# Adjacency layer kernel: row-shaped loads for all tiles, last weights in parts, and four smaller edits

## Chip, cores and metric

The kernel runs on one core of a Trainium2 chip. The metric is the device time of one execution in microseconds (us), as the median of several runs. A core has five engines with queues of their own: PE (TensorE, matrix products), DVE (VectorE), ACT (ScalarE), POOL (GpSimd) and SP (SyncE, which here only issues transfers). Transfers between HBM and the on-chip memory SBUF are carried by 16 DMA engines. Products of PE land in PSUM, which has eight banks of 2 KB a partition.

## What is computed

The reference, cut to what matters. x is (4096, 64), adj is (4096, 4096) with zeros and ones in float32 (64 MiB), and the weight is (64, 64).

```python
h = jnp.maximum(_layernorm(x, axis=-1), 0.0)
support = h @ weight
mask = (adj != 0).astype(support.dtype)
rank = jnp.cumsum(mask, axis=1)
deg = rank[:, -1:]
k = jnp.minimum(deg, 100.0)
pos = rank - (deg - k)
w = mask * jnp.where(pos > 0, 0.5 ** (k - pos), 0.0)
out = x + w @ support + bias
```

A neighbour's weight is thus one half to the power of the number of neighbours that stand behind it in its row, and zero where the row has 100 or more behind it.

## The kernel before

The 4096 rows of adj are cut into 32 tiles of 128 rows (row tile t, one row to each partition, 16 KB a row, 2 MiB a tile). Each goes through a chain of stages, and the tiles overlap in it. The stages, with the function's name, its engine and its line:

1. `load` (SP): row tiles 0 to 29 come as 128 partitions by 16 KB (L307; tile 0 in two halves). Tiles 30 and 31 come "by columns": each of four transfers fills 32 partitions with pieces of 4 KB (L311), twelve transfers in all, since tile 31 is further cut in two.
2. `convert` (DVE, L509) turns the float32 mask into bytes, four to a word. `flip` (DVE, L520 for rows, L525 for columns) transposes 32x32 blocks of words, so that neighbours lie along partitions.
3. `totals` (PE, L532) counts neighbours by blocks, `split` (ACT, L538) takes the two bytes of each count, `suffix` (PE, L551) adds up the counts of the blocks behind with the constant matrices near, rest, far and past. `clamp` (DVE, L556) limits them.
4. `place` (PE, L565 and L570) builds in four PSUM banks (pool v) a word for each neighbour whose bytes are the exponents. `weigh` (ACT, L584) takes the exponential: four instructions a tile, j = 0 to 3, 1024 values a partition each, into the buffer wk, which holds a unit of two tiles.
5. `aggregate` (PE, L601) multiplies hr by a unit's weights: 32 products of 128x256 a unit, in eight tasks of four, accumulated in the one bank of pool acc. hr is the support in two parts, `first` (ACT, L489) and the remainder, `second` (DVE, L492), so that the result has two halves of 64 rows.
6. Every two units (four tiles): `drain` (ACT, L611, for the last part DVE, L613) adds the bias, `turn_back` (PE, L619) transposes 128x128 blocks, `finish` (DVE, L626 and L627) adds the two halves to x in two additions, `store` (SP, L631) writes the rows.

Ahead of the tiles stands a set-up: `fetch` (x), `turn`, `center`, `square`, `relu`, `spread` for the layer norm, `root` (DVE, L462 to L464) and `power` (POOL, L469 to L474, three Newton steps) for the reciprocal root, `support` and `scale` (DVE, L482). `constants` and `order_of` (DVE, L388 to L420) build the constant matrices near, rest, far and where; `count` needs near.

The order on each engine is fixed when the kernel is built. `tasks()` lists every call with its engine, what it needs, how long it holds the engine, and a due time from the table DUE. `plan()` simulates the engines and always takes, of the tasks that can start soon, the one with the smallest due time. The calls are then written out in that order, and every engine works through its own list strictly in order. `pool` entries are PSUM or SBUF buffers: NA = 4 buffers of adj tiles, NV = 5 banks for v, NB = 2 banks for t (which holds tot, ps and po in turn), one bank for acc. A load needs the convert of the tile four before it. `warm` issues products of zeros (L431) where the plan has PE idle before `spread`.

Of the kernel before, what the change touches and what calls it, by code (L numbers as in the profile page):

```python
# [8 lines left out]
F32 = mybir.dt.float32  # L9
# [6 lines left out]
U8 = mybir.dt.uint8  # L16
# [14 lines left out]
UNITS = [("rows", ((t, 0, 4), (t + 1, 0, 4))) for t in range(0, 30, 2)] + [("columns", ((30, 0, 4), (31, 0, 2), (31, 2, 4)))]  # L31
SPANS = {"rows": 8, "columns": 2}
STEP = {0: 2}
U = len(UNITS)
PIECES = [(u, i) for u, (_, pieces) in enumerate(UNITS) for i in range(len(pieces))]
LOADS = []
for u, i in PIECES:
    t, g0, g1 = UNITS[u][1][i]
    step = STEP.get(t, g1 - g0)
    LOADS += [(u, i, k, k + step) for k in range(g0, g1, step)]  # L40
DRAINS = [(g, 0, 4, True) for g in range(7)] + [(7, 0, 2, True), (7, 2, 3, True), (7, 3, 4, False)]
STORES = [(0, 0, 16), (1, 0, 12), (1, 12, 14), (1, 14, 15), (1, 15, 16)]
NA, NM, NT, NW, NV, NB = 4, 4, 4, 2, 5, 2

DUE = {
    "fetch": [-686, -126],
    "load": [724, 583, 273, 792, 448, 655, 939, 650, 1013, 730, -119, 964, 1305, 584, 218, 814, 1129, 955, 149, 993, 40,
    765, 956, 78, 684, 958, 306, 922, 424, 450, 164, 71, 1115, 730],
    "load_rest": [-204],
    "turn": [359, 315, 260, 710, 487, 222, 133, -266],  # L50
    "turned": [-185, -335, 64, -727, -1045, -251, -968, -881],
    "center": [360, -58, 207, -35],
    "square": [-87, -1268, -175, 619],
    "relu": [-239, 514, 1391, -334],
    "spread": [-680, -580, -580, 15],
    "support": [21, 24, 95, 42],
    "scale": [861, -308, -468, -124],
    "root": [844],
    "power": [174],
    "constants": [-220, -1059],  # L60
    "order_of": [1056],
    "count": [1111],
    "counted": [10],
    "first": [-514, -397, -30, -113],
    "second": [-417, 143, 783, 704],
    "convert": [482, 1025, 204, 226, 727, 309, 981, 1114, 367, 687, 1132, 1067, 867, 1749, 1371, 1701, 256, 1583, 1540,
    856, 1257, 1456, 1412, 1612, 1915, 1541, 2485, 1819, 1871, 2184, 1807, 1638, 1616, 2086],
    "flip": [-114, 308, 291, 923, 674, -114, 690, 807, -100, 831, 543, 437, 630, 1887, 1255, 1800, 979, 1228, 961, 744,
    1153, 1971, 1323, 1552, 1990, 1126, 1724, 1289, 2088, 1984, 2223, 1296, 1905, 2123],
    "totals": [-3, 552, -46, 841, 433, 189, 81, 601, 415, -464, -591, 136, 611, 1280, 503, 1008, 578, 335, 987, 424,  # L70
    685, 602, 1305, -158, 1197, 1439, 1190, 839, 1469, 919, 1061, 1251, 1091],
    "split": [761, 727, 1045, 717, 751, 769, -156, 772, 17, 1132, 865, 862, 499, 667, 955, 987, 1510, 1187, 1234, 350,
    1194, 1337, 750, 878, 1289, 1830, 1061, 1369, 1498, 1532, 1176, 1109, 1727],
    "suffix": [183, 405, -150, 111, 631, -317, 930, 770, 128, 167, 1286, 587, 1533, 512, 1005, 852, 704, 676, 956, 1751,
    1680, 1362, 1491, 577, 1388, 1268, 1495, 1814, 1765, 1130, 1431, 1709, 2042],
    "clamp": [321, 347, 443, 415, 222, 598, 567, 424, 121, 506, 857, 749, 466, 653, 638, 701, 1299, 997, 674, -57, 972,
    1295, 1419, 477, 1910, 863, 1576, 1079, 584, 801, 1235, 1277, 1913],
    "place": [-25, 778, 16, 550, 117, -32, 40, -6, 92, 41, -143, 48, 468, -231, -158, 1140, 356, 68, 498, 801, 768,
    1322, 971, 1992, 893, 1057, 834, 1829, 1233, 1823, 1881, 1472, 1293],
    "weigh": [-539, -10, 974, 122, -11, -72, 83, 150, 27, 775, 317, 129, -832, -333, -51, 636, 535, 294, 532, 123, 180,  # L80
    378, 466, -70, 639, 222, 730, 838, 795, 370, 3, 64, 752, 536, 729, 774, 139, 88, 559, 654, 785, 582, 88, 787, 1053,
    118, 807, 706, 489, 825, 591, 69, 761, 655, 427, 704, 340, 743, -9, 457, 789, 281, 1115, 479, 792, 1172, 665, 313,
    1129, 1711, 790, 1140, 1070, 953, 1054, 509, 1453, 384, 1493, 842, 315, 782, 467, 940, 983, 1433, 1265, 954, 1411,
    876, 1666, 1502, 1255, 848, 803, 1220, 1400, 1237, 1021, 1867, 1311, 858, 1342, 1376, 1740, 1425, 1760, 1471, 2210,
    1505, 1441, 1561, 1791, 1838, 1656, 2274, 2036, 1458, 1383, 852, 799, 1464, 848, 1978, 1179, 1428, 1547, 1352, 796,
    2201, 1653, 1588],
    "aggregate": [405, 292, 97, 611, -155, 1241, -31, 842, 332, 334, 1114, 914, 1063, 882, 706, 826, 632, 748, 1116,
    423, 423, 679, 89, 819, 525, 722, 392, 807, 611, 1238, 1392, -269, 1280, 824, 135, 740, 1044, 980, 682, 959, 368,
    650, 826, 977, 447, 432, 945, 564, 860, 911, 943, 1550, 795, 1481, 1191, 503, 690, 693, 824, 516, 1094, 676, 1580,
    2035, 1092, 1330, 876, 1281, 1390, 1259, 1542, 2317, 1637, 1016, 1566, 1168, 1392, 1083, 962, 1526, 1048, 1123,  # L90
    1190, 1017, 661, 1207, 2606, 1891, 1494, 1205, 1663, 1458, 782, 2062, 1503, 2022, 1500, 2071, 2003, 1841, 1219,
    1977, 1613, 827, 1835, 2025, 1748, 1355, 1745, 1953, 2096, 2431, 899, 2009, 1570, 1701, 1819, 1985, 2681, 1641,
    1109, 2260, 2265, 2409, 2272, 1848, 924, 1875],
    "drain": [64, 247, 512, 1185, 1142, 1625, 1534, 1794, 1955, 2201],
    "turn_back": [1333, 1555, 2261, 2462, 2286, 2762, 2419, 1952, 2550, 2777],
    "finish": [403, 912, 821, 1212, 1760, 2467, 1688, 2395, 2803, 2383],
    "store": [10242, 11508, 11343, 11289, 10767],
# [3 lines left out]


def width(u, i):
    _, g0, g1 = UNITS[u][1][i]
    return 64 * (g1 - g0)


def offset(u, i):
    return sum(width(u, k) // 2 for k in range(i))


def tasks():
# [9 lines left out]
    at, when = 6.0, {}  # L122
    for u, i in PIECES:
        at += width(u, i) * 5 / 256
        when[u, i] = at
    for r in range(2):
        task("fetch", (r,), SP, 0.5, 0, 0, [])
    def tile_of(n):
        u, i = LOADS[n][:2]
        return UNITS[u][1][i][0]  # L130

    for n in range(len(LOADS)):
        task("load", (n,), SP, n, 0, 0, [("convert", m) for m in range(n) if tile_of(m) == tile_of(n) - NA])
# [15 lines left out]
    task("power", (), POOL, 3, 2600, 2700, [("root",)])  # L149
    task("constants", (0,), DVE, 0, 600, 650, [])  # L150
    task("constants", (1,), DVE, 6, 1700, 1750, [])
    task("order_of", (), DVE, 1, 1200, 1250, [("constants", 0)])
# [5 lines left out]
    for n, (u, i, k0, k1) in enumerate(LOADS):  # L158
        k = k1 - k0
        due = when[u, i]  # L160
        hold = 622 * k + 20
        task("convert", (n,), DVE, due, hold, hold + 170, [("load", n)], ("b", ("flip", n)))
        hold = 268 * k + (60 if UNITS[u][0] == "rows" else 120)
        o = PIECES.index((u, i))
        task("flip", (n,), DVE, due + 2, hold, hold + 120, [("convert", n)] + ([("place", *PIECES[o - NT])] if o >= NT else []))
    for u, i in PIECES:
        kind, pieces = UNITS[u]
        due, w = when[u, i] + 3, width(u, i)
        task("totals", (u, i), PE, due, 470 * w // 512 + 95, 470 * w // 512 + 315, [("flip", n) for n, part in enumerate(LOADS) if part[:2] == (u, i)], ("t", ("split", u, i)))
        task("split", (u, i), ACT, due + 0.5, 2 * w * 833 // 1000 + 50, 2 * w * 833 // 1000 + 190, [("totals", u, i)])  # L170
        hold = (650 if kind == "rows" else 350) * w // 256
        task("suffix", (u, i), PE, due + 1, hold, hold + 220, [("split", u, i)], ("t", ("clamp", u, i)))
        task("clamp", (u, i), DVE, due + 1.5, w * 1042 // 1000 + 125, w * 1042 // 1000 + 245, [("suffix", u, i), ("counted",)])
        hold = 750 if w == 256 else 650
        task("place", (u, i), PE, due + 2, hold, hold + 220, [("clamp", u, i), ("constants", 1)], ("v", *[("weigh", u, i, j) for j in range(4)]))
        for j in range(4):
            hold = 4 * w * 833 // 1000 + 52
            needs = [("place", u, i)] + ([("second", j) for j in range(4)] if u == 1 else [])
            task("weigh", (u, i, j), ACT, due + 3 + j, hold, hold + 140, needs, ("w", ("aggregate", u, 7)) if i == j == 0 else None)
# [68 lines left out]
def kernel(  # L248
# [9 lines left out]

    nc = tc.nc
    P = 128
# [415 lines left out]
```

## Time and profile before

| what | us |
|---|---|
| median of 3 runs | 198.77 (198.32 to 198.81) |
| the profiled execution, own time | 200.25 |
| its span in the profile | 198.0 |
| PE busy | 164.3 |
| ACT busy | 153.3 |
| DVE busy | 152.1 |
| POOL busy | 9.9 |
| q1, the queue of the loads and stores, share of 16 DMA engines | 88.0% |

The span is the stretch that the profile's records cover; the execution's own time holds 2.25 us more around it. Busy times of an engine count its instructions from start to end, and neighbouring instructions overlap by some tenths of a us, so that four weigh instructions of 1.05 us mean take 3.77 us in a row. The mean granted clock of PE over the span is 0.914 of full speed.

### The profile page before, as it was taken

How to read it: one execution, taken by the hardware profiler on the slowest of the kernel's cores; microseconds unless marked ns; L12 is line 12 of the kernel's file. 1: busy time of each engine (PE TensorE's matmuls, PEld its weight loads, DVE VectorE, ACT ScalarE, POOL GpSimd, SP SyncE). 2: the span in 40 equal slices, each digit the busy share in tenths (PEclk: the TensorE clock that was granted, in tenths of full speed). 3: DMA queues.
4: the chain of work that ended last, by engine and by line, in shares of the span. 5: the costliest groups of instructions: out<-in, count | busy, mean ns of one | idle time of the engine just before them, and what ended most of it. 6: DMA issues, size and time to landing. Idle time of an engine off the chain costs nothing.

```text
span 198.0 us, 4612 instructions
## 1 busy us (share of the span) xinstructions
PE 164.3 (83%) x2007; PEld 124.3 (63%) x2007; DVE 152.1 (77%) x169; ACT 153.3 (77%) x195; POOL 9.9 (5%) x46
## 2 busy tenths in 40 slices
PE   7899882698965998898988898998988978568992
PEld 5775571386753776676666776785866755445881
DVE  4876869996996988979988689999989845664212
ACT  2863468385938997999999999989999996286650
POOL 7000820000000000000000000000000000000000
PEclk9995599559999999999999999999999996965899
DMA  6999999999999999999999999999999999830020
GB/s 221 405 434 424 440 424 406 437 427 427 427 420 424 422 430 420 427 424 434 424 424 417 430 417 427 427 430 424 430 417 391 199 223 223 243 118 3 0 93 13
DMA packets 6947, 69.52 MB, mean 351 GB/s; under 512 B 1296, under 2 KB 1424, under 8 KB 2960
## 3 DMA queue, kind: packets, MB, share of 16 engines
q1 hardware_dynamic: 6768, 69.21, 88.0%
q8 instruction: 15, 0.25, 0.5%
q10 hardware_dynamic: 160, 0.03, 0.1%
q14 instruction: 4, 0.03, 0.1%
HBM read 68.19 MB, written 1.05 MB: 350 GB/s over the span
## 4 chain that ended last, share of the span: by engine, by line
PE 37%; DMA 22%; DVE 17%; ACT 15%; POOL 3%; issue 3%; SPq 1%; POOLq 0%; ACTq 0%; DVEq 0%
PE acc L601 22%; DMA a_sb<-in_adj_dram 22%; ACT wk L584 12%; DVE m L509 8%; PE ps L551 5%; DVE mt L520 4%; PE v L570 3%; PE v L565 3%; PE tot L532 3%; DVE behind L556 2%; POOL t L473 2%; ACT sums L538 1%; PE po L619 1%; ACT acc_sb L611 1%; DVE wk L482 1%
## 5 line engine op out<-in xcount | busy, mean ns | idle before, releaser
L584 ACT ACTIVATE wk<-v 128x1024 fp32r<-128x1024 uint8 (+1 forms) x132 | 123.0, 1029 | 13.7 <-PE v L570 12.6
L509 DVE TENSOR_SCALAR m<-a_sb 128x4096 uint8<-128x4096 f32 (+1 forms) x34 | 84.0, 2479 | 13.4 <-DMA a_sb<-in_adj_dram 13.4
L601 PE MATMUL acc<-wk,hr 128*128 128x256 f32 x512 | 78.1, 304 | 6.2 <-ACT wk L584 5.4
L601 PEld LDWEIGHTS acc<-wk,hr 128*128 128x128 f32 x512 | 68.6, 203 | 14.6 <-ACT wk L584 7.6
L520 DVE STREAM_TRANSPOSE mt<-m 128x1024 f32<-128x1024 f32 (+1 forms) x31 | 37.1, 1203 | 0.3
L538 ACT ACTIVATE sums<-tot 128x512 f16<-128x512 uint8 (+1 forms) x33 | 20.0, 607 | 14.2 <-PE tot L532 7.8
L556 DVE TENSOR_SCALAR behind<-ps,excess 128x256 f16<-128x256 f32 (+1 forms) x33 | 15.5, 470 | 19.0 <-PE ps L551 17.1
L565 PE MATMUL v<-behind,where 32*128 32x256 f16 (+1 forms) x264 | 16.8, 281 | 12.1 <-DVE behind L556 8.7
L532 PE MATMUL tot<-mt,band 128*32 128x256 f16 (+1 forms) x264 | 14.3, 300 | 4.6 <-DVE mt L520 3.1
L551 PEld LDWEIGHTS <-far_rows 128*128 128x128 f16 x210 | 17.3, 103 | 1.2
L565 PEld LDWEIGHTS <-where 32*128 32x128 f16 x264 | 5.9, 93 | 19.2 <-issue 16.5
L551 PE MATMUL ps<-sums,far_rows 128*128 128x224 f16 (+6 forms) x210 | 17.8, 228 | 0.0
L570 PE MATMUL v<-mt,tri 32*32 32x512 f16 (+1 forms) x528 | 15.3, 413 | 0.0
L551 PE MATMUL ps<-sums,near 128*128 128x256 f16 (+1 forms) x33 | 9.7, 293 | 4.7 <-ACT sums L538 4.6
L532 PEld LDWEIGHTS <-band 128*32 128x32 f16 x264 | 4.4, 97 | 11.4 <-issue 5.3
L570 PEld LDWEIGHTS <-tri 32*32 32x32 f16 x528 | 4.6, 88 | 7.2 <-issue 7.0
L551 PE MATMUL ps<-sums,rest_rows 128*128 128x256 f16 x30 | 8.6, 287 | 0.0
L611 ACT ACTIVATE acc_sb<-acc,bias_sb 128x512 f32<-128x512 f32 (+2 forms) x9 | 5.8, 644 | 2.8 <-PE acc L601 2.7
L551 PEld LDWEIGHTS <-near 128*128 128x128 f16 x33 | 3.5, 105 | 5.6 <-issue 3.4
L458 PEld LDWEIGHTS pd<-ones,wk 128*128 128x128 f32 x32 | 5.0, 234 | 1.8 <-ACT wk L449 1.3
L619 PE MATMUL po<-ident,acc_sb 128*128 128x128 f32 x31 | 5.1, 282 | 1.0 <-ACT acc_sb L611 1.0
L449 ACT ACTIVATE wk<-pc 128x512 f32<-128x512 f32 x4 | 2.4, 600 | 4.6 <-PE pc L446 4.6
(93 smaller groups left out, 87.7 us busy)
## 6 DMA issues: line engine op xcount, KB each, us to landing
a_sb<-in_adj_dram SPq DMA_DIRECT2D x29, 2048.0 KB, 13.8
a_sb<-in_adj_dram SPq DMA_DIRECT2D x2, 1024.0 KB, 8.6
a_sb<-in_adj_dram SPq DMA_DIRECT2D x4, 512.0 KB, 19.1
a_sb<-in_adj_dram SPq DMA_DIRECT2D x8, 256.0 KB, 11.9
xr<-in_x_dram SPq DMA_DIRECT2D x2, 512.0 KB, 3.8
out_dram<-xr SPq DMA_DIRECT2D x1, 512.0 KB, 7.4
out_dram<-xr SPq DMA_DIRECT2D x1, 384.0 KB, 2.3
out_dram<-xr SPq DMA_DIRECT2D x1, 64.0 KB, 1.7
```

What stands on the lines that cost most here:

```text
L509: nc.vector.tensor_scalar(m_v, a_v, 0.0, 64.0, op0=ALU.not_equal, op1=ALU.add)
L520: nc.vector.transpose(to.rearrange("p c (h r) -> p h c r", r=SUB)[:, 2 * k0:2 * k1], m_v)
L532: nc.tensor.matmul(tot[SUB * c:SUB * (c + 1), :w], band[:, SUB - 12 - 4 * a:2 * SUB - 12 - 4 * a], masks[u, i][:, c, :w, a], start=(a == 0 ...
L538: nc.scalar.activation(sums8[u, i][:, :, :w], pts.pop((u, i, "n"))[:, :w].bitcast(U8).rearrange("p (i f) -> p f i", f=4)[:, :2, :], AF.Cop ...
L551: nc.tensor.matmul(o, l, m, start=(k == 0), stop=(k == len(todo) - 1), skip_group_check=True)
L556: nc.vector.tensor_scalar(behind[u, i][:, :w], pts.pop((u, i, "s"))[:, :w], excess, float(MAX_NEIGH), op0=ALU.subtract, op1=ALU.min)
L565: nc.tensor.matmul(vs[u, i, j][:, a * w:(a + 1) * w], where[q, a, :], behind[u, i][q, :w], start=(a == 0), stop=False, skip_group_check=True)
L570: nc.tensor.matmul(vs[u, i, j][SUB * c:SUB * (c + 1), :2 * w], tri[q, q], masks[u, i][q, c, :w, :].rearrange("p i a -> p a i"), start=Fals ...
L584: nc.scalar.activation(to, v, AF.Exp, scale=-LN2, bias=-38.0 * LN2)
L601: nc.tensor.matmul(accs[g][:, at:at + 2 * P], hr[:, b, :, :].rearrange("p s d -> p (s d)"), w, start=(k == m == 0), stop=(k == 7 and m == ...
L611: nc.scalar.activation(sums[d][:, :w], accs[g][:, i0 * P:i1 * P], AF.Identity, bias=bias_sb)
L619: nc.tensor.transpose(pts["o", d][:, k, :, :].rearrange("p s d -> p (s d)"), sums[d][:, k * P:(k + 1) * P], ident)
```

## The change

Six things differ.

- All 32 tiles are loaded by rows. Tiles 0, 1 and 28 to 31 come in two halves of 1 MiB (8 KB a row), the others whole. The column form goes with everything that served it: L311, the second form of flip, rest and far in two versions.
- The weights of tile 31 are made in three parts: for each j one instruction of 512 values, then one of 256, then one of 256 (PARTED), and the aggregates of the last unit each need only the part that they read. An aggregate task now takes one (a, s) and four h.
- `power` moves from POOL to DVE, nine instructions in place of thirteen. `constants(1)` and `order_of` move from DVE to POOL.
- `warm` is called ahead of any task: where the plan has PE idle and PE's recent work in a stretch of 3.4 us is small, products of zeros are put in, which add nothing to the accumulator in use.
- `turn_back` multiplies by the matrix `both` (two identities of 64 on top of each other), which transposes and adds the two halves in one product, so `finish` is one addition. The last drains and stores are cut in two pieces in place of three, and all drains are on ACT.
- Buffers: NV = 6 and NB = 1 in place of 5 and 2; two buffers for sums in place of one. The table DUE is new, and so is the order on every engine.

```diff
-UNITS = [("rows", ((t, 0, 4), (t + 1, 0, 4))) for t in range(0, 30, 2)] + [("columns", ((30, 0, 4), (31, 0, 2), (31, 2, 4)))]
-STEP = {0: 2}
-DRAINS = [(g, 0, 4, True) for g in range(7)] + [(7, 0, 2, True), (7, 2, 3, True), (7, 3, 4, False)]
-STORES = [(0, 0, 16), (1, 0, 12), (1, 12, 14), (1, 14, 15), (1, 15, 16)]
-NA, NM, NT, NW, NV, NB = 4, 4, 4, 2, 5, 2
+TILES = range(32)
+STEP = {t: 4 for t in (0, 1, 28, 29, 30, 31)}
+LOADS = [(t, h, h + STEP.get(t, 8)) for t in TILES for h in range(0, 8, STEP.get(t, 8))]
+PARTLY = {31}
+PARTED = (0, 1, 0, 2), (1, 2, 0, 1), (1, 2, 1, 2)
+DRAINS = [(g, 0, 4, True) for g in range(7)] + [(7, 0, 2, True), (7, 2, 4, True)]
+STORES = [(0, 0, 16), (1, 0, 12), (1, 12, 14), (1, 14, 16)]
+NA, NM, NT, NW, NV, NB = 4, 4, 4, 2, 6, 1
...
     def load(n):
...
-        if kind == "rows":
-            nc.sync.dma_start(tiles[t][:, k0 * N // 4:k1 * N // 4], adj_v[:, t // HT, t % HT, k0 * N // 4:k1 * N // 4])
-        else:
-            to = tiles[t].rearrange("(q p) (g n) -> q p g n", q=E, g=E)
-            for q in range(E):
-                nc.sync.dma_start(to[q, :, k0:k1, :], quarters[t // HT, t % HT, q, :, k0:k1, :])
+        nc.sync.dma_start(tiles[t][:, k0 * W:k1 * W], adj_v[:, t // HT, t % HT, k0 * W:k1 * W])
...
     def power():
         y, t, v = ns["y"], ns["t"], ns["v"]
-        nc.gpsimd.tensor_scalar(v, v, -0.5, None, op0=ALU.mult)
         for i in range(3):
-            nc.gpsimd.tensor_tensor(t, y, y, op=ALU.mult)
-            nc.gpsimd.tensor_tensor(t, t, v, op=ALU.mult)
-            nc.gpsimd.tensor_scalar(t, t, 1.5, None, op0=ALU.add)
-            nc.gpsimd.tensor_tensor(y, y, t, op=ALU.mult)
+            nc.vector.tensor_tensor(t, y, y, op=ALU.mult)
+            nc.vector.scalar_tensor_tensor(t, v, -0.5, t, op0=ALU.mult, op1=ALU.mult)
+            nc.vector.scalar_tensor_tensor(y, t, 1.5, y, op0=ALU.add, op1=ALU.mult)
...
+    idle = [ps_a.tile([P, W], F32, tag="acc", name="none"), 2 * P]
     def warm(n):
-        for i in range(n):
-            nc.tensor.matmul(none[:, :2 * P], junk[:, :P], junk, start=True, stop=True)
+        for i in range(n if idle else 0):
+            nc.tensor.matmul(idle[0][:, idle[1]:idle[1] + 2 * P], junk[:, :P], junk, start=not accs, stop=not accs, skip_group_check=True)
...
-    def weigh(u, i, j):
+    def weigh(t, j, part=0):
...
+        a0, a1, s0, s1 = PARTED[part] if t in PARTLY else (0, 2, 0, 2)
+        v = vs[t, j].rearrange("p a i -> p (a i)").bitcast(U8).rearrange("p (x r f) -> p f x r", f=4, r=SUB)
+        nc.scalar.activation(wts[u][:, s0:s1, 8 * a0:8 * a1, i, j, :], v[:, s0:s1, 8 * a0:8 * a1], AF.Exp, scale=-LN2, bias=-38.0 * LN2)
...
     def turn_back(d):
...
-            nc.tensor.transpose(pts["o", d][:, k, :, :].rearrange("p s d -> p (s d)"), sums[d][:, k * P:(k + 1) * P], ident)
+            nc.tensor.matmul(pts["o", d][:, k, :], sums[d][:, k * P:(k + 1) * P], both, start=True, stop=True)
...
     def finish(d):
...
-        nc.vector.tensor_add(o, po[:, :i1 - i0, 0, :], o)
-        nc.vector.tensor_add(o, po[:, :i1 - i0, 1, :], o)
+        nc.vector.tensor_add(o, pts.pop(("o", d))[:, :i1 - i0, :], o)
...
-    end = 1200
-    for at, hold, on_pe, f, args in plan():
-        if on_pe:
-            if end is not None and at - end > 700:
-                warm(int(at - end) // 215)
-            end = None if f == "spread" or end is None else at + hold
+    for at, spare, f, args in plan():
+        warm(spare)
         does[f](*args)
```

In plan(), the number of zero products ahead of a PE task:

```python
idle = 0
if engine == PE:
    recent = sum(rows for when, rows in spent if when > at - 3400)
    idle = max(0, min(int((at - end) * 0.6) // 110, (4200 - recent) // 256))
    spent += [(at, rows_of(f, args) + 256 * idle)]
    end = at + hold
```

## The prediction

> **What bounds the kernel now.** I read the slices first, for stages. One slice is 4.95 us.
>
> ```profile
> PEclk9995599559999999999999999999999996965899
> DMA  6999999999999999999999999999999999830020
> GB/s 221 405 434 424 440 424 406 437 427 427 427 420 424 422 430 420 427 424 434 424 424 417 430 417 427 427 430 424 430 417 391 199 223 223 243 118 3 0 93 13
> ```
>
> The reader is to see two things: all 16 DMA engines are busy to slice 36, but from slice 32 they move half as much, and behind the last byte lie four and a half slices with no load at all. The windows put numbers to it (columns: PE, PEld, DVE, ACT, POOL busy us and instructions, granted clock, DMA share, GB/s):
>
> ```profile
> 0.00:150.00 150.00, 128.84 (x1591) 96.27 (x1591) 127.75 (x137) 121.77 (x153) 9.93 (x46) 0.93 1.00 418
> 150.00:177.00 27.00, 20.66 (x254) 16.08 (x249) 18.02 (x16) 20.56 (x25) 0.00 (x0) 0.89 0.91 231
> 177.00:198.00 21.00, 14.80 (x168) 11.99 (x167) 6.36 (x17) 10.95 (x19) 0.00 (x0) 0.81 0.08 27
> ```
>
> Stage one: 150 us of stream at 418 GB/s (425 once it runs, in 60 to 150 us). Stage two: 27 us at 231 GB/s. Stage three: 21 us of work behind the last load. The queue of SP issues its first transfer by columns (L311) at 146.87, just before the rate falls. Next, VectorE's timeline, for when data is taken up: L509 converts a tile as soon as it may.
>
> ```profile
> 59.55 2.63 DVE L509 TENSOR_SCALAR m<-a_sb 128x4096 uint8<-128x4096 f32 x1
> ...
> 116.25 2.64 DVE L509 TENSOR_SCALAR m<-a_sb 128x4096 uint8<-128x4096 f32 x1
> ...
> 149.16 2.61 DVE L509 TENSOR_SCALAR m<-a_sb 128x4096 uint8<-128x4096 f32 x1
> ...
> 161.03 2.63 DVE L509 TENSOR_SCALAR m<-a_sb 128x4096 uint8<-128x4096 f32 x1 [3.24 <-DMA a_sb<-in_adj_dram]
> ...
> 169.90 2.63 DVE L509 TENSOR_SCALAR m<-a_sb 128x4096 uint8<-128x4096 f32 x1 [3.95 <-DMA a_sb<-in_adj_dram]
> ...
> 177.30 1.37 DVE L509 TENSOR_SCALAR m<-a_sb 128x2048 uint8<-128x2048 f32 x1 [1.91 <-DMA a_sb<-in_adj_dram]
> ```
>
> These are tiles 9, 20, 27, 29, 30 and the last half of 31. Between 22 and 157 us no convert waits for data; from tile 29 on each does. Last, the chain of waits (start, us, what), which names the end:
>
> ```profile
> 148.19 21.58 DMA a_sb<-in_adj_dram
> 169.79 7.38 DMA a_sb<-in_adj_dram
> ...
> 177.30 1.37 DVE m L509
> ...
> 189.54 4.07 PE acc L601 x32
> ```
>
> So what sets the end is the arrival of the last two tiles, and then a tail of 198.0 - 177.3 = 20.7 us.
>
> **The change, part by part.** *(1) Rows in place of columns.* The 12 transfers of L311 go; tiles 28 to 31 come in eight of 1 MB with 8 KB rows. By 150 us 150 x 0.418 = 62.7 MB are in; adj and x are 68.2 MB (the page's HBM read). The other 5.5 MB at 425 GB/s take 12.9 us: all bytes by 162.9. Landing is seen later than bytes: tile 1 is complete by bytes at 14.7 us and its convert, waiting for nothing else, starts at 16.7. With 0.5 to 2 us the last half lands at 163.4 to 164.9; I take 164.5, as the end of a queue has nothing behind it to share with. The nearest row for 8 KB rows is tile 0, two such halves: 5 to 15 us moved 408 and 447 GB/s, the full rate.
>
> The Trainium skill speaks against it here ("SBUF — State Buffer", The DMA setup-cost knee): a transfer of 1 MiB alone reaches some 330 to 340 GB/s, since each pays a fixed cost of about 2 us. By that rule the last 8 MB would take 8.4 / 0.335 = 25.0 us and not 19.7, an estimate of 5.3 us more; the row shows queued halves without such a loss.
>
> *(2) When VectorE gets to it.* Tile 20 is complete at 1.05 + 21 x 2.097 = 45.1 MB; by the windows' rates 41.5 are in by 100 us and 426 GB/s follow, so its bytes were there at 108.5, 7.8 us before its convert; those of tile 27, the same way, at 143.0, 6.1 before. Over these 7 tiles the converts came every 4.70 us and the DMA every 4.93, so 0.23 a tile is recovered. Four tiles more leave 5.2: the last convert at 162.9 + 5.2 = 168.1 by this, at 164.5 by landing alone. I take the middle, 166.3, since halves let a convert begin before its tile is whole, and keep both ends.
>
> *(3) The tail, from the last convert's start.* VectorE: convert 1.37, clamp of tile 30 0.40, turn 0.71: 2.5. Totals 0.34 and signals: 2.95. ScalarE has one weigh of tile 30 in front (0.94, back to back, from 3.77 for four), split 0.50 net: 4.1. Suffix 0.65 behind one group of four products 0.60: 5.4. Clamp 0.48: 5.9. Place 0.75 behind another group: 6.9, when ScalarE has done tile 30's other three weighs too. Then weights in parts: four of 512 elements at 0.52 (2.10 for four at the end of before): 9.0; a drain 0.50; eight of 256 elements. No row has 256; 0.94 for 1024 and 0.52 for 512 make a straight line, 0.31, bounds 0.21 and 0.52: 9.5 + 2.5 = 12.0. In parts ScalarE spends 0.18 more for each j, 0.7 in all, but 24 of the unit's 32 products run under it; without parts all 32 (4.07 above) would follow. After the last part 8 products x 0.127 = 1.0, drain 0.50, two products turn back 0.44, one addition 0.29, signals 0.2: 14.5. From the last store's issue at 195.4 to the end before took 2.6, and stays.
>
> *(4) Zero products.* 87 in place of 20 in the built order of PE; 74 stand ahead of the first aggregate, 13 later. One is 0.14 us (5 in 0.70) warm, 0.215 at the start. The 13 cost at most 1.8 us, if none falls into a gap; PE idles 3.6 us in 105 to 150 alone. Their gain: the clock is 0.50 in 15 to 20 and 35 to 45 us, where aggregates take 4 in 1.0 and not 0.5. Both lie in the stage the stream covers, so 0; if the cover is gone, -3 to +2.
>
> *(5) Roots on VectorE.* 13 operations on POOL (19.88 to 26.50, 6.6 us) go; 9 on VectorE come, by L462 to L464 (0.18 to 0.19) 1.7 us. Queued behind them are tile 2's convert and all that follows; VectorE idled 0.51 and 1.49 us in just that stretch. Scale may start 4 us sooner, but the halves of hr (L492) are ordered behind tile 5's turn. Zero in the sum; -1 to +1.
>
> *(6) Constants on POOL.* 19 small operations (4.3 us, 4.40 to 8.7) leave VectorE, which then waited for data anyway: 0. POOL gets 24 at some 0.3 (as its 128x32 rows take) and gaps of 0.07: 8.9 us, from 5.6 to 14.5; the first suffix needs near, at 19.2 before. Against it stands one row pair:
>
> ```profile
> 22.17 2.64 POOL L473 TENSOR_SCALAR t<-t 128x32 f32<-128x32 f32 x1
> ...
> 22.02 2.67 DVE L509 TENSOR_SCALAR m<-a_sb 128x4096 uint8<-128x4096 f32 x1 [0.51 <-DMA a_sb<-in_adj_dram]
> ```
>
> A POOL operation of 0.3 lasted until the convert beside it ended. Four half converts lie in 9 to 18 us: up to 4 x 1.37 = 5.5, near at 20.0, 0.8 late, still under the stream: 0 in the sum, up to +1.
>
> The Trainium skill ("SBUF — State Buffer", Who interferes with whom) makes this a rule: VectorE and GpSimd share a port pair, and the one that comes second is blocked for the other's whole instruction. By it I would book the 0.8, by the other twelve root operations (0.24 to 0.30) nothing.
>
> *(7) One addition of halves; banks.* finish loses 0.42 x 7 on VectorE and 0.3 at the end (in the sum of 3); the product with both is no longer than the transposition it replaces (0.15). The t pool has one bank in place of two, v six for five. In VectorE's order clamp(t) stands ahead of the turn of t + 1 for 20 of 31 tiles, so totals(t + 1) could not have come sooner there; for 11 it can wait up to a convert (2.6), and 9 turn_backs take the bank some 1 us each. ScalarE's and PE's queues stand behind. Hidden while a tile's own work stays under 4.93 us; -0 to +4 for the end.
>
> Sum: 166.3 + 14.5 + 2.6 = 183.4 of span. The profiled execution took 200.25 for a span of 198.0, so 185.65 on its own scale; the median 198.77 is 1.48 below that: **184.2**.
>
> **The rivals.** *A, the stream as above*, 180.8 to 188: for it, the fall of the rate at the first column transfer; against it, the lag in (2). *B, the engines set the pace.* Tiles 9 to 20 came every (116.25 - 59.55) / 11 = 5.15 us, slower than the stream. 22 tiles from 59.55 so: the last half at 175.5, end 192.6 of span, 193.4. For it, ScalarE busy 42.6 of 45 us in 60 to 105; against, 4.70 later. *C, the rate falls at the end whatever the shape.* Only the shorter tail remains: 20.7 - 17.1 = 3.6, so 195.2; against it, L311's timing. *D, slower: the single t bank.* One tile's chain through it is 0.34 + 0.50 + 0.65 + 0.48 and signals 0.3 = 2.3; with a weigh (0.94), two groups of products (1.2) and a convert (2.6) in front of each step, 7.0 a tile. A gain of 14.6 over 31 tiles is gone from 4.93 + 0.47 = 5.4 us a tile; with ScalarE's and VectorE's waits always, 5.9: 31 x 0.97 = 30 later, 214. Against it, the 20 of 31.
>
> **How the numbers follow.** A 0.70, B 0.17, C 0.05, D 0.08. The likeliest gives 184.2. Low end: landing alone (-1.8), parts at the low bound and a warm tail (-1.6): 180.8. High end: A with 168.1 and half of the bank's 4, 188.0, then into B to leave out 0.2 in all: 190.5. Within 0.3% is about what runs of this kernel cannot tell apart (198.32 to 198.81). Faster: A, B and most of C, 0.90; same 0.02; slower, D, 0.08.
>
> **What would show it.** Right: no 4 KB column transfers, 420 or more in every slice to 33, last convert at 164.5 to 168, tail near 17, clock 9 at 35 to 45 us. B: converts later than 170 with no wait for data. C: slices at 220 again. D: totals and turn_back waiting for clamp and finish, converts over 5.4 us apart. Wrong altogether if the start of the span (constants on POOL) pushes the first weights past 30 us.

## The result, and the profile after

| what | before | after |
|---|---|---|
| median, us (range, runs) | 198.79 (198.32 to 198.92, 4) | 188.63 (188.37 to 189.29, 4) |
| ratio after to before | | 0.9498, 95% interval 0.9469 to 0.9528 |
| profiled execution, us | 200.25 | 188.37 |
| its span, us | 198.0 | 186.7 |
| mean granted clock of PE | 0.914 | 0.973 |
| start of the last convert, us | 177.30 | 167.35 |
| from there to the issue of the last store, us | 18.1 | 16.7 |

The change is 10.2 us faster where 14.6 were forecast; 188.63 lies within the range, 4.4 us above the predicted time. Executions that ran over 1.5% above the fastest of their kernel are left out of all ratios. First the slices of the changed kernel (40 equal ones of 4.67 us, counted from 0: granted clock, busy share of the DMA engines, GB/s).

```profile
PEclk9997569999999999999999999999999999999999
DMA  6999999999999999999999999999999999940020
GB/s 202 390 427 435 435 420 425 416 428 428 428 414 428 434 414 432 428 414 442 411 428 428 418 432 421 418 446 411 428 421 414 413 420 416 417 201 0 12 90 16
```

The four slices at 199 to 243 GB/s are gone, and so is the second dip of the clock at 35 to 45 us (in a second profile of the same kernel, further down, 3.4 us of half clock remain from 42.2). Now the end of the stream closer (columns as in the windows shown before).

```profile
150.00:160.00 10.00, 9.18 (x130) 7.33 (x128) 9.44 (x11) 9.98 (x13) 0.00 (x0) 1.00 1.01 418
160.00:162.00 2.00, 1.32 (x33) 0.59 (x33) 2.00 (x3) 2.00 (x3) 0.00 (x0) 1.00 1.00 414
162.00:164.00 2.00, 2.00 (x22) 1.94 (x21) 1.97 (x3) 2.00 (x4) 0.00 (x0) 1.00 0.97 401
164.00:166.00 2.00, 2.00 (x44) 1.30 (x40) 2.00 (x4) 1.98 (x4) 0.00 (x0) 1.00 0.65 262
166.00:168.00 2.00, 2.00 (x24) 1.84 (x17) 1.97 (x3) 2.00 (x3) 0.00 (x0) 1.00 0.18 74
```

The queue does not end at one moment: the busy share of the DMA engines falls over the last four us, 0.65 and then 0.18. Two things overlap there. A store stands behind the last load in the same queue (512 KB, issued at 150.54, landed 17.1 us later). By the records of the single packets, the first of its 128 packets of 4 KB starts at 162.45, while the last packet of the load (8 KB) ends at 165.90; after that only the store moves, until 167.16. A packet of the load takes 0.31 us to the very end, as in 150 to 160 us. So the engines do not get slower; some are through with their part of the load, and with the store behind it, up to 3.4 us before others (an inference, as the records do not name the engine). VectorE's last four converts:

```profile
161.03 1.35 DVE L496 TENSOR_SCALAR m<-a_sb 128x2048 uint8<-128x2048 f32 x1
163.05 1.36 DVE L496 TENSOR_SCALAR m<-a_sb 128x2048 uint8<-128x2048 f32 x1
165.31 1.38 DVE L496 TENSOR_SCALAR m<-a_sb 128x2048 uint8<-128x2048 f32 x1
167.35 1.36 DVE L496 TENSOR_SCALAR m<-a_sb 128x2048 uint8<-128x2048 f32 x1
```

None waits for data any more; before, tiles 29, 30 and the last half of 31 waited 3.24, 3.95 and 1.91 us. The chain that ended last says the same. Its shares of the span by engine, before and then after:

```profile
PE 37%; DMA 22%; DVE 17%; ACT 15%; POOL 3%; issue 3%; SPq 1%; POOLq 0%; ACTq 0%; DVEq 0%
ACT 36%; PE 32%; DVE 15%; POOL 10%; issue 5%; POOLq 0%; ACTq 0%
```

After the change no transfer stands in the chain: the engines are about a us behind the stream, whose last packet of the load ends at 165.90. (Where a convert waits for it, in the run with the constants on VectorE below, it starts 0.45 us after that packet.) Then the tail, PE's timeline behind the place of tile 31 (start, us, instruction, idle time before it and what ended it):

```profile
174.41 0.45 PE L542 MATMUL v<-mt,tri 32*32 32x512 f16 x16
174.78 1.10 PE L580 MATMUL po<-both,acc_sb 128*128 128x64 f32 x8
175.70 1.66 PE L559 MATMUL acc<-wk,hr 128*128 128x256 f32 x12
177.99 0.74 PE L559 MATMUL acc<-wk,hr 128*128 128x256 f32 x4 [0.62 <-ACT acc_sb L572]
178.56 0.55 PE L580 MATMUL po<-both,acc_sb 128*128 128x64 f32 x4
178.92 3.56 PE L559 MATMUL acc<-wk,hr 128*128 128x256 f32 x28
183.10 0.66 PE L580 MATMUL po<-both,acc_sb 128*128 128x64 f32 x4 [0.62 <-ACT acc_sb L572]
```

and ScalarE's beside it:

```profile
171.98 5.02 ACT L551 ACTIVATE wk<-v 128x1024 fp32r<-128x1024 uint8 x7
177.46 0.47 ACT L572 ACTIVATE acc_sb<-acc,bias_sb 128x256 f32<-128x256 f32 x1 [0.46 <-PE acc L559]
177.83 2.31 ACT L551 ACTIVATE wk<-v 128x256 fp32r<-128x256 uint8 x8
182.58 0.47 ACT L572 ACTIVATE acc_sb<-acc,bias_sb 128x256 f32<-128x256 f32 x1 [2.44 <-PE acc L559]
```

The weights are all made at 180.14, yet PE's last product ends at 182.48. PE came to the last unit late: it first turned group 6 back (1.10), did the last twelve products of unit 14, then stopped 0.62 for a drain. From the end of place (174.86) to the last product 7.6 us pass, and PE is the one that is behind.

### The profile page after: what moved, and what is told of

It reads as the page before. It is cut to its first block, busy times and chain, and to the rows that moved or that the text cites. A ratio compares the mean times of both kernels' runs of the same rounds, so it can differ in the third digit from the quotient of the medians.

```text
span 186.7 us, 4747 instructions
## 1 busy us (share of the span) xinstructions
PE 164.9 (88%) x2080; PEld 127.3 (68%) x2080; DVE 146.8 (79%) x152; ACT 152.1 (82%) x198; POOL 18.9 (10%) x57
## 3 DMA queue, kind: packets, MB, share of 16 engines
HBM read 68.19 MB, written 1.05 MB: 371 GB/s over the span
## 4 chain that ended last, share of the span: by engine, by line
ACT 36%; PE 32%; DVE 15%; POOL 10%; issue 5%; POOLq 0%; ACTq 0%
ACT wk L551 29%; PE acc L559 19%; DVE m L496 7%; ACT sums L517 5%; PE ps L526 5%; PE po L580 3%; DVE mt L506 3%; PE v L542 2%; DVE behind L530 2%; PE v L538 2%; PE tot L512 2%; ACT acc_sb L572 1%; DVE wk L472 1%; DVE hr L482 1%; POOL where L414 1%
## 5 line engine op out<-in xcount | busy, mean ns | idle before, releaser
L551 ACT ACTIVATE wk<-v 128x1024 fp32r<-128x1024 uint8 (+2 forms) x136 | 123.2, 1028 | 2.3 <-PE v L542 2.1
L517 ACT ACTIVATE sums<-tot 128x512 f16<-128x512 uint8 x32 | 20.3, 634 | 16.4 <-PE tot L512 16.4
L530 DVE TENSOR_SCALAR behind<-ps,excess 128x256 f16<-128x256 f32 x32 | 15.4, 481 | 14.1 <-PE ps L526 13.9
L526 PEld LDWEIGHTS <-far 128*128 128x128 f16 x224 | 17.9, 101 | 1.9 <-POOL far L389 1.0
L526 PE MATMUL ps<-sums,far 128*128 128x224 f16 (+6 forms) x224 | 18.5, 225 | 0.7 <-POOL far L389 0.7
L512 PE MATMUL tot<-mt,band 128*32 128x256 f16 x256 | 13.5, 288 | 5.3 <-DVE mt L506 4.3
L538 PE MATMUL v<-behind,where 32*128 32x256 f16 x256 | 13.6, 276 | 2.7 <-DVE behind L530 2.3
L542 PE MATMUL v<-mt,tri 32*32 32x512 f16 x512 | 14.5, 401 | 0.0
L423 PE MATMUL none<-junk 128*128 128x256 bf16 x74 | 11.9, 318 | 1.1 <-DVE junk L307 1.1
L526 PE MATMUL ps<-sums,near 128*128 128x256 f16 x32 | 9.2, 286 | 2.0 <-ACT sums L517 1.8
## 6 DMA issues: line engine op xcount, KB each, us to landing
out_dram<-xr SPq DMA_DIRECT2D x1, 512.0 KB, 17.1
```

Source lines behind the costliest of these rows:

```text
L423: nc.tensor.matmul(idle[0][:, idle[1]:idle[1] + 2 * P], junk[:, :P], junk, start=not accs, stop=not accs, skip_group_check=True)
L512: nc.tensor.matmul(tot[SUB * c:SUB * (c + 1), :V], band[:, SUB - 12 - 4 * a:2 * SUB - 12 - 4 * a], masks[t][:, c, :, a], start=(a == 0), s ...
L517: nc.scalar.activation(sums8[t], pts.pop((t, "n"))[:, :V].bitcast(U8).rearrange("p (i f) -> p f i", f=4)[:, :2, :], AF.Copy, bias=-136.0)
L526: nc.tensor.matmul(o, l, m, start=(k == 0), stop=(k == len(todo) - 1), skip_group_check=True)
L530: nc.vector.tensor_scalar(behind[t], pts.pop((t, "s"))[:, :V], excess, float(MAX_NEIGH), op0=ALU.subtract, op1=ALU.min)
L538: nc.tensor.matmul(vs[t, j][:, a, :], where[q, a, :], behind[t][q, :], start=(a == 0), stop=False, skip_group_check=True)
```

## The experiments

The medians of before on other chips lay between 198.9 and 200.0 us, so each run is read by its ratio to before on its own chip; the changed kernel's own is 0.944 to 0.950.

**Rows alone.** Before, with tiles 30 and 31 by rows and nothing else changed.

```diff
-UNITS = [... for t in range(0, 30, 2)] + [("columns", ((30, 0, 4), (31, 0, 2), (31, 2, 4)))]
-STEP = {0: 2}
+UNITS = [... for t in range(0, 32, 2)]
+STEP = {0: 2, 31: 2}
```

> The kernel before with one part of the change alone: tiles 30 and 31 by rows, tile 31 in two halves; order table, banks, set-up and everything else as before. Theory S (the stream by columns cost most of the gain): 420 GB/s or more in every slice to 33, no convert of tiles 29 to 31 waits for data by more than 1 us, last convert near 167 to 170, time 188 to 192. Rival R (the other five edits made the gain): 195 or more. Rival C of the prediction (the rate falls at the end whatever the shape): slices near 220 again, 196 to 199.

Measured 193.90 (193.19 to 195.44), ratio 0.9711 (0.9626 to 0.9797): 5.8 us under before. The rate is 414 to 432 GB/s in slices 28 to 33, and the last half is taken up at 168.1, 9.2 us sooner. But the span shrinks by 6.7 only, since the tail grew. PE's timeline of that run:

```profile
180.68 1.22 PE L601 MATMUL acc<-wk,hr 128*128 128x256 f32 x4 [2.75 <-ACT acc_sb L611]
...
181.98 4.42 PE L601 MATMUL acc<-wk,hr 128*128 128x256 f32 x28
```

When data came late, PE had nothing to do at its arrival (it waited 2.55 us, to 179.08), and ScalarE soon after (1.60, to 180.37). Now they have a backlog, the drain comes behind all weights, PE waits 2.75 us for it, and the 28 products run at a mean clock of 0.78 (4.42 us; in the changed kernel 3.56 at 1.00). So the rows give a little over half of the gain. Of the 4.6 us of span between this run and the changed kernel (191.3 and 186.7), 0.8 lie ahead of the last convert's start and 3.8 behind it, in the tail.

**What makes a transfer slow: partitions or short rows.** In the changed kernel, tiles 30 and 31 once in transfers of 32 partitions with rows of 8 KB, once in transfers of 128 partitions with pieces of 4 KB.

```diff
+            for q in range(4):
+                nc.sync.dma_start(tiles[t][q * SUB:(q + 1) * SUB, k0 * W:k1 * W], adj_v[q * SUB:(q + 1) * SUB, t // HT, t % HT, k0 * W:k1 * W])
```

> The changed kernel, but tiles 30 and 31 arrive in transfers of 32 partitions each, with rows of 8 KB as in the changed kernel. Theory W (the number of partitions that a transfer reaches sets the rate): about 220 GB/s for the last 4.2 MB, the last half lands 4.2/0.22 - 4.2/0.425 = 9 us later, near 174, and of these 9 us the 3 that VectorE lagged are absorbed: 194 to 198. Rival P (the 4 KB pieces set it): 420 GB/s to the end, 188 to 190.

```diff
+            for k in range(k0, k1, 2):
+                nc.sync.dma_start(tiles[t][:, k * W:(k + 2) * W], adj_v[:, t // HT, t % HT, k * W:(k + 2) * W])
```

> The changed kernel, but tiles 30 and 31 arrive in transfers of 128 partitions with pieces of 4 KB (512 KB each). Theory W: 420 GB/s to the end, 188 to 190. Rival P: about 220 GB/s for the last 4.2 MB, 194 to 198.

Quarters: 199.39 (197.54 to 200.86; the profiled execution 200.61), ratio 0.9983 (0.9939 to 1.0028). Pieces: 188.84 (188.76 to 189.00), ratio 0.9434 (0.9375 to 0.9493). The rates by slices, of the quarters:

```profile
GB/s 235 402 435 433 428 400 384 425 438 422 425 432 423 415 425 432 418 435 422 428 422 425 418 418 435 418 442 422 410 412 390 229 214 242 242 77 0 3 92 13
```

and of the pieces:

```profile
GB/s 211 404 431 443 406 436 354 422 438 424 424 431 424 419 421 431 431 417 424 442 414 421 431 421 431 421 421 435 424 417 417 414 416 405 412 227 0 27 77 14
```

With 32 partitions the rate halves again, with rows of 8 KB as before with 4 KB; pieces of 4 KB in transfers of 512 KB cost nothing. The whole gain hangs on this one property: with it undone, all other edits, in the order made for the fast stream, leave no gain. The Trainium skill names a reason ("SBUF — State Buffer", Door 1: The DMA port swizzle): 32 neighbouring partitions reach eight of sixteen ports, which it puts at about 218 GB/s. The quarters moved 229 in 155 to 175 us, 5% more. That ports are the reason no run here tests; the runs separate only the number of partitions from the row length.

**Zero products.** Only those ahead of turn and center stay, 23 in place of 87.

```diff
-        warm(spare)
+        if f in ("turn", "center"):
+            warm(spare)
```

> The changed kernel with zero products ahead of the turn and center tasks alone (23), none in later gaps. If they keep the clock up: the granted clock shows 0.5 somewhere in 25 to 50 us, the first aggregates are slower, and by theory A, since ScalarE waits there, 0.5 to 2 us more: 189 to 190.5. If they do nothing (my sum): 188.4 to 189. If they cost PE time: less than 188.4.

Measured 191.16 (191.11 to 191.56), ratio 0.9571 (0.9511 to 0.9632). The changed kernel was not run on this chip; against its median elsewhere that is 2.5 us more, by the ratios 1.5 to 2.6, and the span of the profiled execution is 3.1 longer. The granted clock and the last convert:

```profile
PEclk9998559655599999999999999999999999999998
```

```profile
170.59 1.35 DVE L496 TENSOR_SCALAR m<-a_sb 128x2048 uint8<-128x2048 f32 x1
```

The clock is at half speed again from 34.7 to 51.8 us (slices 8 to 10 wholly). The convert that starts at 58.85 in the changed kernel starts at 62.13 here, 3.3 late; the same ones later start at 86.47 against 83.29, 111.28 against 108.10, 137.14 against 133.94 and 170.59 against 167.35. A delay of the early stage is carried to the end almost whole, although the stream runs at 424 GB/s meanwhile (60 to 150 us).

**Weights of tile 31 in one part.**

```diff
-PARTLY = {31}
+PARTLY = set()
```

> The changed kernel with the weights of tile 31 in one instruction for each j, as for other tiles. If the tail is bound by PE's queue behind the last place (1.1 of turn_back, 12 products of the unit before, a wait for the drain, 32 products: 7.7 us), parts bring little: 188.6 to 190. If parts hide most of the 32 products behind the weights, as my sum had it: 2 to 3.5 us more, 191 to 192.

Measured 189.44 (188.98 to 189.53), ratio 0.9476 (0.9416 to 0.9537): 0.8 us by the medians, but the ratio lies within the changed kernel's own 0.944 to 0.950, and in the trace the tail is 17.0 for 16.7. The parts save little, as PE and not ScalarE is behind in the tail.

**Constants on VectorE**, by the code of before, the rest as after.

```diff
-        task("constants", (1,), POOL, 6, 4500, 4600, [("constants", 0)])
-        task("order_of", (), POOL, 1, 3500, 3600, [("constants", 0)])
+        task("constants", (1,), DVE, 6, 2150, 2200, [])
+        task("order_of", (), DVE, 1, 2150, 2200, [("constants", 0)])
```

> The changed kernel with the constant matrices built on VectorE again, by the code of before. near is then ready near 9.5 us in place of 19.4, the first suffix no longer waits, and hr is ready some 3 us sooner than 46.0. Theory A (from about 46 us ScalarE is never without work, so the end is the start of its run plus its work): the weights of tile 2 start 3 us sooner and the time falls by 2 to 3.5, to 185 to 186.5. Rival D (the stream's landing sets the end, a late start is caught up): 188.0 to 189.

Measured 187.74 (186.79 to 189.33), ratio 0.9414 (0.9324 to 0.9505). The weights of tile 2 begin at 44.04 in place of 46.09, and the last convert is:

```profile
166.63 1.36 DVE L491 TENSOR_SCALAR m<-a_sb 128x2048 uint8<-128x2048 f32 x1 [0.34 <-DMA a_sb<-in_adj_dram]
```

So two us sooner at the start became 0.7 at the end, because there VectorE waits for the data: this is where the stream's own bound lies. The chain that ended last is now mostly transfers again:

```profile
DMA 55%; DVE 24%; PE 15%; ACT 2%; issue 1%; ACTq 0%
```

In the median it is 0.9 us, less than the runs differ, and under the 2 to 3.5 of theory A.

**The remainders of hr early**, so that the weights of tile 2 can start.

```diff
-    "second": [869, 310, 488, 149],
+    "second": [-3000, -3000, -3000, -3000],
```

> The changed kernel with one due time altered: the remainders of hr (second) go as soon as they can, ahead of the converts of tiles 4 and 5; the constants stay on POOL. The weights of tile 2 start near 40 in place of 46.1 us. Theory A: 3 to 5 us less, 183.5 to 185.5, until the landing of the last half (near 165) and the tail set it. Rival D: 188.0 to 189.

The weights of tile 2 begin at 40.68 and not 46.09, and nothing comes of it: 188.87 in the profiled execution, last convert at 167.95. The four executions took 188.80, 188.87, 191.66 and 192.33; the ratio 0.9451 (0.9359 to 0.9542) is of the first two. ScalarE meets waits of 1.2 to 1.6 us at 65, 128 and 139 us in place of its late start. Its start and its work alone don't set the end.

**Where PE loses time in the tail.** Four kernels of one chip: the changed kernel itself, the same with the drain of the first half of the last group behind all products of the last unit's weights, this together with the constants on VectorE, and the changed kernel with two t banks.

> The changed kernel itself, on the same chip as the three runs beside it, as their reference. Theory: ratio 0.944 to 0.952 as before, and a tail (last convert's start to last store's issue) of 16.5 to 17 us, whatever the chip. Rival: the tail shape was of one execution; then PE's order of waits at the end differs.

188.59 (188.25 to 188.84), ratio 0.9441 (0.9406 to 0.9477). Last convert 167.60, last store's issue 16.7 later, with the same waits of 0.62 and 0.46, as the theory has it.

```diff
-    "drain": [82, 374, 29, 620, 400, 1392, 1843, 1544, 1599],
+    "drain": [82, 374, 29, 620, 400, 1392, 1843, 9000, 9100],
...
-        task("turn_back", (d,), PE, ..., [("drain", d)], ("t", ("finish", d)))
+        task("turn_back", (d,), PE, ..., [("drain", d)] + ([("aggregate", 15, 7)] if d == 7 else []), ("t", ("finish", d)))
```

> The changed kernel with one wait taken out of the tail: ScalarE drains the first half of the last group behind the weights of tile 31, not between their first and second part, and PE adds up all of the last unit before it turns that half back. Theory T (PE's queue and the drain that ScalarE waits for, 0.46 us, and that PE then waits for, 0.62 us, set the tail): the weights are done at 179.3 in place of 180.1, PE has its twelve products of unit 14 done at 177.2 and goes on without a stop, 32 x 0.127 = 4.1, so 181.3 in place of 182.5; then one drain, four turns: 1.0 to 1.4 us less, tail 15.3 to 15.8. Rival U (the tail is set by what ScalarE does before, and the two drains and turns at the end cost what is won): within 0.4 us of the changed kernel.

188.63 (188.28 to 188.90): no gain, the rival's number. But the trace shows why, and it is not the rival's reason:

```profile
175.63 4.03 PE L559 MATMUL acc<-wk,hr 128*128 128x256 f32 x32
180.28 1.69 PE L559 MATMUL acc<-wk,hr 128*128 128x256 f32 x12 [0.62 <-ACT acc_sb L572]
181.80 0.55 PE L580 MATMUL po<-both,acc_sb 128*128 128x64 f32 x4
182.98 0.66 PE L580 MATMUL po<-both,acc_sb 128*128 128x64 f32 x4 [0.62 <-ACT acc_sb L572]
```

PE went on without a stop at 177, and stopped twelve products from the end instead: the drain and the products share the bank acc, and in both places of the drain in the order the products behind it wait 0.62 us for it. The wait is for ScalarE's signal, so the program asks for it; whether the chip would need it is not shown. The weights were done at 179.1. A wait was moved, not removed.

The same tail with the constants on VectorE:

> The tail of the run above and, besides, the constants on VectorE as in the kernel before. If the two gains are independent (1.0 to 1.4 and some 0.9): 1.9 to 2.3 us under the changed kernel, 186.3 to 186.8 on its scale. Rival: the constants' gain was of the chip or of one execution, and only the tail's remains: 1.0 to 1.4 less, the last convert at 167.3 and not 166.6.

187.84 (187.38 to 189.06), ratio 0.9418 (0.9379 to 0.9458). Last convert 167.42, after a wait of 0.35 for data. 0.75 us under the changed kernel in the median, with ranges that overlap: unclear.

**A bank of its own for the last unit**, with the constants on VectorE.

```diff
+        if u == 15:
+            g = 8
         if g not in accs:
-            accs[g] = ps_a.tile([P, W], F32, tag="acc", name="acc")
+            accs[g] = (ps_v.tile([P, W], F32, tag="v", name="acc2") if g == 8 else ps_a.tile([P, W], F32, tag="acc", name="acc"))
...
-            nc.scalar.activation(sums[d][:, :w], accs[g][:, i0 * P:i1 * P], AF.Identity, bias=bias_sb)
+            nc.scalar.activation(sums[d][:, :w], accs[d if d == 8 else g][:, i0 * P:i1 * P], AF.Identity, bias=bias_sb)
...
-        task("turn_back", (d,), PE, ..., [("drain", d)], ("t", ("finish", d)))
+        task("turn_back", (d,), PE, ..., [("drain", d)] + ([("aggregate", 15, 5)] if d == 7 else []), ("t", ("finish", d)))
```

> Constants on VectorE, and the products of the last unit summed in a bank of their own (one of the v pool's), so that no product has to wait for the drain of the first half, which stood in the same bank; the first half is turned back behind 28 of the 32 products. Theory V (it is the shared bank that stops PE at the end: 0.62 us wherever the drain stands, as in the run with the late drain): no wait of a product of L559's kind for acc_sb; from the end of place of tile 31: 0.9 turns, 1.5 for twelve, 28 x 0.127, 0.4 turns, 0.5: 6.9 to the last product in place of 7.7, tail 15.8 to 16.1, and with the constants' 0.8 some 1.6 us under the changed kernel: ratio 0.934 to 0.939. Rival (ScalarE's last parts are then what PE waits for): the last products start behind the last part at 5.4 and end at 6.5 to 6.9 as well, but PE shows a wait for wk; or no gain, ratio 0.941 to 0.945.

PE's tail in this run:

```profile
174.35 5.23 PE L556 MATMUL acc<-wk,hr 128*128 128x256 f32 x40
179.42 0.55 PE L577 MATMUL po<-both,acc_sb 128*128 128x64 f32 x4
179.78 0.72 PE L556 MATMUL acc<-wk,hr 128*128 128x256 f32 x4
181.12 0.66 PE L577 MATMUL po<-both,acc_sb 128*128 128x64 f32 x4 [0.62 <-ACT acc_sb L569]
```

The 40 products run in one piece; no product waits for acc_sb or wk. The last convert starts at 166.62 and the last store is issued at 182.1: a tail of 15.5 where the changed kernel has 16.7. The profiled execution took 186.58, the shortest of all. The median, 188.06 (186.58 to 188.69), has a ratio of 0.9486 (0.9448 to 0.9524) on its chip, so that a faster kernel is not shown by the times (0.934 to 0.939 was expected), only a shorter tail by the trace.

**Banks.** The order on every engine as in the changed kernel, with two banks for t and five for v.

```diff
-    ps_t = ctx.enter_context(tc.tile_pool(name="ps_t", bufs=NB, space=bass.MemoryType.PSUM))
-    ps_v = ctx.enter_context(tc.tile_pool(name="ps_v", bufs=NV, space=bass.MemoryType.PSUM))
+    ps_t = ctx.enter_context(tc.tile_pool(name="ps_t", bufs=2, space=bass.MemoryType.PSUM))
+    ps_v = ctx.enter_context(tc.tile_pool(name="ps_v", bufs=5, space=bass.MemoryType.PSUM))
```

> The changed kernel with the order of all engines unchanged, but with two banks for t and five for v. It asks what the single t bank costs, which the prediction bounded by 0 and 4 us. Theory Z (nothing: the engines' orders already put clamp ahead of the next totals, and ScalarE's queue is the limit): the t side gives 0 to -0.5 us, and the sixth v bank, which is now gone, costs 0 to 1.5: 188.4 to 190. Rival Y (the t bank costs the 2 to 4 us that the last convert was late): 185 to 187.5, and the waits of totals and turn_back for clamp and finish are gone.

196.75 (196.11 to 198.91), ratio 0.9844 (0.9804 to 0.9885): 8.2 us slower than the changed kernel beside it, and outside both theories. The waits (who waited for whom: us in total, times, longest), of this run:

```profile
ACT sums L517 <- PE tot L512: 23.2, 15, 6.5
...
PE v L538 <- ACT wk L551: 8.1, 15, 1.1
```

and of the changed kernel on the same chip:

```profile
ACT sums L517 <- PE tot L512: 17.1, 6, 6.5
...
PE po L580 <- DVE behind L530: 1.2, 2, 0.7
PE tot L512 <- DVE behind L530: 0.8, 2, 0.6
PE v L538 <- ACT wk L551: 0.2, 1, 0.2
```

With five banks place waits for the weights of the tile before, 15 times, 8.1 us in all: one tile holds four, so with five the next tile finds one bank free and with six two. From 60 to 144 us the converts come every 5.60 us and no longer every 5.0. The single t bank, which made room for the sixth, costs the 1.2 and 0.8 us of PE in the lines with behind, which are gone here. Whether five banks would cost as much in an order made for five was not tried.

## Why the prediction was right, and where it was short

Direction and the main mechanism held: with rows the last data come 10 us sooner, and the time is rival A's, 0.6 us above its upper end of 188. But what ended last was not the stream. It was the engines, as in rival B, about a us behind it, and no transfer stands in the chain. The sum was 166.3 + 14.5 + 2.6 = 183.4 of span; measured 167.35 + 16.75 + 2.6 = 186.7. The miss of 4.4 is 1.05 in the second step, 2.25 in the third, and 1.1 in the step from span to median. Of the signs named for being right, the last convert and the clock came; some slices lay at 411 to 418 where 420 was the least, and the tail to the end of the span was 19.3 and not near 17.

*(1) Rows.* Right in the rate (413 to 428 GB/s in the slices from 28 to 34), and right in the cause, as quarters and pieces show. Wrong in the landing: 163.4 to 164.9 was taken with "the end of a queue has nothing behind it to share with". A store does stand behind it, and the load's own end thins out: 114 of its packets, 0.93 MB, start after 162 us, which at 424 GB/s would be in by 164.2 and not 165.90. Where converts wait for the last half they start at 166.6 to 167.7, 2 to 3 us later than taken, and no order tried here gets under 166.6. A run with that store later was not made; as the packets keep their 0.31 us, nothing in the trace lays the delay on the store. The setup-cost rule of the Trainium skill ("SBUF — State Buffer", The DMA setup-cost knee), 5.3 us by the prediction's estimate, does not show in this queue: transfers of 1 MiB and, in the pieces, of 512 KB ran at 405 to 428 GB/s.

*(2) VectorE.* 167.35 for 166.3, within 164.5 to 168.1, though by another way. The lag was not recovered by 0.23 a tile: in the changed kernel converts came every 5.0 us from 59 to 134, slightly slower than the stream's 4.93. That the sum is only 1.05 off is luck: the stream's end was late for one reason and the engines for another, and the two met. (A small slip of the reading before: of the last converts there, the first half of tile 31 did not wait.)

*(3) The tail*, 14.5, is the term that was mis-sized most: 16.75. The parts were costed well (0.29 each of 256 elements for 0.31 taken), and their effect was not: "24 of the unit's 32 products run under it" failed. PE was not free: 1.10 for group 6's turns and 1.66 for twelve products of unit 14 stood in its queue, and the drain of the shared bank stopped it for 0.62. 28 products were left at 178.92, not 8 at the end of the weights. Of the 2.25, 0.8 were there when the weights were done (180.14), the rest came with these products. The run in one part (little lost), the moved drain (nothing won) and the own bank (a tail 1.2 shorter) show this one after another.

*From span to median.* Before's profiled execution was 1.48 above its median, and I took this off. The changed kernel's profiled execution lies 0.26 below its median instead. The clock that dips in the gaps (0.89 and 0.81 in the last two stages of before) is a possible cause of the excess and is gone, but this is not shown: executions of before at mean clocks of 0.90 to 0.94 took 197.3 to 201.3 us in no clear order. The excess of one execution of the old kernel said nothing of the new one.

*(4) Zero products*, booked at 0, are worth some 2.5 us. The cover named for it, the stream, was thin: VectorE is paced by the engines from 60 us on, and gives back almost nothing. This gain offset part of the misses, which was luck: without them 191.16 would have been above the range's 190.5. The bounds -3 to +2 for a missing cover held.

In 30 to 50 us the run with few zero products has a mean clock of 0.62 and the changed kernel 1.00. The trace's records of the granted clock show steps: in all runs the recorded stretches that end inside the span are whole multiples of 3.41 us, here 17.07 at half clock from 34.71 on. It fell while PE was idle for 3.04 us (32.67 to 35.71). The Trainium skill ("TensorE: Matmul & The Clock Gate", Part 1) gives an idle window of about 3.4 us for the fall to half clock. The length of the steps agrees; but the 3.41 us ahead of the fall were not idle throughout, as PE worked to 32.67.

*(5) Roots on VectorE* took 2.0 us of it (nine operations, 23.05 to 25.03) for the 1.7 costed. Not separated by a run.

*(6) Constants on POOL.* near was ready at 19.42 (20.0 at worst), but all 24 operations only at 21.62, where 14.5 was expected. The first suffix needs far as well, which the prediction left out: PE stopped 0.72 us for it, and that suffix ended 2 us later than before. POOL's timeline shows operations beside the converts:

```profile
8.65 1.99 POOL L411 TENSOR_SCALAR more<-idx,row 128x256 f32<-128x256 f32 x1
...
14.05 1.44 POOL L377 TENSOR_SCALAR sub<-pf,sub 128x1 f32<-128x1 f32 x1
```

and VectorE's:

```profile
9.03 1.37 DVE L496 TENSOR_SCALAR m<-a_sb 128x2048 uint8<-128x2048 f32 x1 [3.93 <-DMA a_sb<-in_adj_dram]
...
14.01 1.39 DVE L496 TENSOR_SCALAR m<-a_sb 128x2048 uint8<-128x2048 f32 x1 [0.37 <-DMA a_sb<-in_adj_dram]
```

An operation on one element a partition, 0.2 us else, lasts 1.44, to the end of the convert beside it. Four were stretched so, and others took longer than the 0.3 booked (0.4 to 1.2 for those on 128 or 256 elements). VectorE then waits 1.83 us for the count and 1.31 for the first suffix; the run without it gained 0.9 in the median, within the spread of its runs, near the "up to +1".

*(7) Banks.* Rival D did not come: the single t bank shows 2.0 us of waits on PE. What the prediction left unpriced is the other half of the trade. "v six for five" carries the pace: without it, in this order, 8.2 us. Rival C falls by the slices. B falls by its number, 193.4, and by the converts at the end, which come every 4.3 us a tile, faster than the stream; but the tile pace of 5.0 us and the missing wait for data are its share of the truth.

What stays open: how the some 5 us between rows alone and the whole change add up. Only the zero products (some 2.5) stand clear of the spread; the parts (0.8) and the constants (0.9 back) do not. The rest lies in the new order, the sixth bank, the roots and the single addition, which were not taken apart, and as the order differs the pieces need not add.

## What to carry to other kernels

When a load that sets the end is made faster, write out the queue of every engine behind it, PE too: work that hid in the old wait becomes the tail, and a wait in a shared bank can move with the drain rather than go away. Call a stage covered only after comparing the paces per tile; at 5.0 us against the stream's 4.93 a delay at 50 us arrives at 170. And price both sides of a trade of buffers, for the one gained can be worth far more than the one given up.

## What was not expected of the hardware

- A load over 16 DMA engines ends unevenly: after 401 GB/s, two us at 262 and two at 74, part of it already the store behind. The first packet of that store starts 3.4 us before the last one of the load ends, though each packet of the load takes its usual 0.31 us.
- The granted clock changes only after multiples of 3.41 us, and half clock can last although PE has work: 17.07 us in the run with few zero products, where PE was busy 8.7 of the 14 us from 38 to 52. With 64 small products more, 9 us of work at 0.14, none (one profile) or 3.41 us (the other) of it is left there.
- 32 partitions at a time halve the rate (229 GB/s against 418) with rows of 8 KB as with 4 KB; short rows alone, over 128 partitions, do not.
